# A graph layer on one core: from which chunk ScalarE and SyncE take over single gathers from GpSimd

## The chip, the cores and the metric

The kernel runs on one core of a Trainium2 chip. Its time is the device time of one launch in microseconds, as the median of the runs shown; before the change that is 15449.47 us (three runs, 15443.1 to 15450.64 us). The engines are named as the profile names them: PE (TensorE, matrix products), DVE (VectorE), ACT (ScalarE), POOL (GpSimd) and SP (SyncE, which only issues transfers here).

## The reference

A graph of 50,000 nodes with 160 features each and 1,650,000 edges, sorted by target. Each edge takes the row of its source node, multiplies it with four edge attributes and small weight matrices, and is summed into its target; then follow a residual, a ReLU and a layer norm.

```python
ss, vv = (s[src], v[src])                       # rows of the source nodes
out0 = C0 * (ss * e0 @ W1 + dot * INV3 @ W2)
out1 = C1 * (p3 + p4 + p5)                      # linear in the source row, too
m = jnp.concatenate([out0, out1.reshape(-1, 3 * MUL1)], axis=1)
m_agg = jax.ops.segment_sum(m, dst, num_segments=n)
...
return x + jax.nn.relu(h)                       # h: m_agg times Ws and Wv
x = _layernorm(x + _L0_gnn_ref(...), axis=-1)
```

Everything ahead of the ReLU is linear in the source rows, so the kernel first sums the rows times each of the four attributes (160 features times 4) and multiplies with one folded matrix per node afterwards.

## The kernel before

**Units, groups, pairs, chunks.** 128 edges are a unit, 6 units a group, 2 groups a pair (12 units), 10 pairs a chunk (120 units). There are 1044 pairs in 105 chunks, which the code numbers from 0, so the seventh chunk is chunk 6 and the third is chunk 2. Chunks 0 to 4 read their edges from the inputs; chunk 5 and later read them from a table `edges` in DRAM that the kernel writes itself, free of self loops.

**The way of a unit.** POOL gathers its 128 source rows with one indirect transfer (`gather`, line 459) into `xg`, a buffer of one pair, of which there are four (pool `rows`). So POOL can start pair p + 4 only when PE has done pair p. DVE builds the weighted one-hot matrices `ha` (`spread`, lines 474 and 477), PE multiplies (line 502), and DVE adds the result to the node sums (`turn_sums`, lines 518 and 527). When 128 nodes are complete, PE multiplies them with the folded matrix (line 822), DVE adds the residual rows `xt` and norms (lines 185 to 201), ACT takes a square root (line 195), SP loads `xt` ahead (line 765) and sends the result (line 920).

**Single rows.** Some units of a chunk are not gathered by POOL. A `Fetcher` of an engine fetches their 128 rows with 128 plain transfers of 640 bytes (line 376), whose addresses it loads into registers 32 at a time (line 372). `spots` holds the places in a chunk: units 38 and 98 for ACT, 104 for SP, before the change in chunks 2 to 103. DVE prepares the addresses (`list_rows`, lines 403 and 404). The rows of chunk s + 1 are handed out evenly (`deal`) over ten pairs from the fifth pair of chunk s on, so these transfers stand in the orders of ACT and SP between their other work. ACT writes into `xscalar`, SP into `xsync`.

**Packs.** The table `edges` is made in packs of 128 table rows, beside the main loop. SP reads a pack's edges (`read`, lines 596 to 600); ACT casts them to `prow` (`begin`, lines 604 to 606) and, three times, a third of the sources to `marks` (`count`, line 624); DVE marks and moves out self loops (lines 625 to 688); SP stores the table, in 16 rounds of 8 rows of 28,440 bytes (`edges<-prow`, each with 768 bytes `selves<-mine`; line 739, addresses loaded at line 722) and a short last round. There is one buffer `prow`: the cast that begins a pack waits until all stores of the pack before have landed. The first pack has to be stored before chunk 5 is loaded; later packs have some 1,400 us each.

**What sets the order.** On SP, PE, DVE and ACT the order of the code holds (`manual_schedule`), each engine waits in order, and work that belongs to a later pair is put in between the groups by `after_pair` and `work`; a pack's steps are spread evenly up to a due pair. Of eight semaphores, SP's other transfers each take the next one and wait until its last transfer has landed; single rows have their own semaphores and don't wait.

Of the kernel before, what the change touches and what calls it, by code (L numbers as in the profile page):

```python
# [39 lines left out]
F32 = mybir.dt.float32  # L40
I32 = mybir.dt.int32
# [3 lines left out]
ALU = mybir.AluOpType  # L45
AX = mybir.AxisListType
ET = mybir.EngineType
# [3 lines left out]
P = 128  # L51
MUL0, MUL1 = 64, 32
D = MUL0 + 3 * MUL1
# [10 lines left out]
W = 32  # L64
# [3 lines left out]
PG = 2  # L68
# [9 lines left out]
KM = WS - 1  # L78
REST = 15
LEAD = 3  # L80
BY_SCALAR, BY_SYNC = 2, 1
FBEGIN, FWAIT = 4, 4

def plan(n_nodes, n_edges):

    nblk = 125
    assert n_nodes % nblk == 0
    assert W == FB
    nb = n_nodes // nblk
    again = 9  # L90

    per_unit = P * n_nodes / n_edges
    group = max(g for g in range(1, 17)
                if g == 1 or (g + 0.2) * per_unit + 1 + 5 * math.sqrt(g * per_unit * per_unit / P) <= W)
    head = math.ceil(min(HEAD, n_edges / (group * P)) / SG) * SG
    eh = head * group * P
    row = group * P * 3 // 2 + math.floor(per_unit * group * 3 / 2 * (1 - n_nodes / n_edges))
    assert row * n_nodes / n_edges + 5 * math.sqrt(row * n_nodes / n_edges / 16) < KM

    far = math.ceil(6 * math.sqrt(n_edges) / 2 * n_nodes / n_edges) + 2  # L100
    rows = math.ceil((n_edges - eh) / row) + 2
    ngroups = math.ceil((n_edges - n_nodes + eh * n_nodes / n_edges + far) / (group * P))
    assert eh + (rows - 1) * row - n_nodes + eh * n_nodes / n_edges - far >= ngroups * group * P
    units = P * math.ceil(max(math.ceil(n_edges / P) + again - 1, math.ceil((eh + rows * row + 1) / P)) / P)
    return nblk, nb, again, group, units, ngroups, row, head, rows, far
# [3 lines left out]
def tile_gnn_resnorm(ctx: ExitStack, tc: tile.TileContext, x, src, dst, attr, W1, W2, W3, W4, W5, Ws, Wv, out, n_edges):  # L109
    nc = tc.nc  # L110
    N = x.shape[0]
    NBLK, NB, GA, G, NU, NG, L, NH, NR, FAR = plan(N, n_edges)
# [107 lines left out]
    NSC = math.ceil(NG / SG)  # L220
# [12 lines left out]
    with tc.tile_pool(name="once", bufs=1) as once, tc.tile_pool(name="raw", bufs=2) as rawp, \  # L233
# [8 lines left out]
        spotp, ownp, listp, heldp, scalarp, syncp = (  # L242
            later_pools.enter_context(tc.tile_pool(name=name, bufs=bufs))
            for name, bufs in (("spot", 3), ("own", 2), ("list", 2), ("held", 1),
                               ("scalar", BY_SCALAR + 1), ("sync", BY_SYNC + 1)))
        extremes = once.tile([P, 2, NSC], F32, name="extremes")
        count_ = once.tile([1, SG], F32, name="count")
        nc.gpsimd.iota(count_, pattern=[[1, SG]], base=0, channel_multiplier=0, allow_small_or_imprecise_dtypes=True)
# [8 lines left out]
        per = SG // PG  # L257
# [92 lines left out]

        class Fetcher:

            def __init__(self, engine, et, pool, n, place):
                self.engine, self.et, self.pool, self.n = engine, et, pool, n
                self.rows, self.turn, self.left, self.asked = deque(), 0, 0, []
                self.landed = [tc.alloc_semaphore(f"{pool.name}{i}") for i in range(4 * (n + 1))]
                self.spots = [math.ceil((FBEGIN + per * (i + 1) / n + FWAIT - per) * PG * G) + place for i in range(n)]
                assert all(0 <= at < per * PG * G for at in self.spots)

            def prepare(self, s, line, at, u):  # L360

# [19 lines left out]

                self.rows.extend(partial(one, q, e) for q in range(P // W) for e in range(W))

            def begin(self, wanted):
                assert len(self.rows) == wanted * self.n * P
                self.left = len(self.rows)

            def deal(self, gone):
                keep = math.floor(P * self.n * (1 - gone))
                while self.left > keep:  # L390
                    self.rows.popleft()()
                    self.left -= 1

        fetchers = [Fetcher(*f) for f in ((nc.scalar, ET.Activation, scalarp, BY_SCALAR, 2), (nc.sync, ET.SP, syncp, BY_SYNC, 8)) if f[3]]
        wanted = [(f, at) for f in fetchers for at in f.spots]
        assert len({at for _, at in wanted}) == len(wanted)

        def list_rows(s, u0, ef):

            line = listp.tile([P, len(wanted), W], I32, name="line")  # L400
            held = heldp.tile([P, len(wanted), W], F32, name="held")
            for i, (f, at) in enumerate(wanted):
                nc.vector.tensor_scalar(held[:, i], ef[:, 0, (u0 + at) % NK], 0.0, float(N - 1), op0=ALU.max, op1=ALU.min)
            nc.vector.tensor_scalar(line, held, float(4 * D), None, op0=ALU.mult)
            for i, (f, at) in enumerate(wanted):
                f.prepare(s, line[:, i], at, u0 + at)

# [436 lines left out]
        spots = once.tile([1, 2 * npacks * RP], I32, name="spots")  # L844
# [10 lines left out]
        counts = once.tile([P, 2, npacks], F32, name="counts")  # L855
# [9 lines left out]
        def after_pair(p, f, *args):  # L865
            later.setdefault(p, []).append((f, args))
# [96 lines left out]
        def reach(s):  # L963

            end = min(NG, (s + 1) * SG) * G * P
            if s * SG < NH:
                return 0
            if s + 1 < NSC:
                end = max(end, (s * SG * G + P) * P)
            if s * SG == NH:  # L970
                end = max(end, (s * SG + W) * G * P)
            return end - EH

        packs, due = [], []
        for i in range(npacks):

            first = next(s for s in range(NH // SG, NSC)
                         if reach(s) > row_start(i * RP)[0][0])
# [23 lines left out]
        for p, (s, g, ng) in enumerate(pairs):  # L1002
            if (p + LEAD) % per == 0 and (p + LEAD) // per + 1 < NSC or not p:
                ahead_ = (p + LEAD) // per + 1
                end = reach(ahead_)
                assert end <= 0 or rows_stored[0] == NR or end <= row_start(rows_stored[0])[0][0]
                raws[ahead_] = load(ahead_)
            if p % per == 0 and s + 1 < NSC:
                after_pair(p + 1, do_cast, s + 1)
                after_pair(p + 2, do_place, s + 1)  # L1010
                if s + 2 == NSC:
                    after_pair(p + 4, examine_all)
                    after_pair(p + 6, read_flags)
            rows = gather(s, placed[s], (g - s * SG) * G, ng * G)
            for j, ps in enumerate(group_sums(p, rows, has.pop(p))):
                if j == 1 and turning:
                    turn_sums(*turning)
                    turning = None
                if j == 3 and p + 1 < len(pairs):
                    s1, g1, ng1 = pairs[p + 1]  # L1020
                    has[p + 1] = spread(placed[s1], (g1 - s1 * SG) * G, ng1 * G)
                work(1.0)
                if p % per == FBEGIN and not j:
                    begun_at = p
                    for f in fetchers:
                        f.begin(0 < s < NSC - 2)
                for f in fetchers:
                    if f.left:
                        f.deal((p - begun_at + (j + 1) / (ng * G)) / per)
                if packs and p >= START:  # L1030
                    when = p + (j + 1) / (ng * G)
                    todo = math.ceil(len(packs[0]) * min(1, (when - began) / max(1, due[0] - began)))
                    for step in packs[0][done:todo]:
                        if step:
                            step()
                    done = max(done, todo)
                    if done == len(packs[0]):
                        packs.pop(0), due.pop(0)
                        done, began = 0, when
            turning = p, ps  # L1040
            if p == START - 2:
                with ExitStack() as behind, tc.tile_pool(name="begin", bufs=1) as beginp:
                    for i in first_ones:
                        behind.enter_context(tc.issue_after(i))
                    weights(beginp, psM)
            if p == START - 1:
                with ExitStack() as behind, tc.tile_pool(name="table", bufs=1) as tablep:
                    for i in first_ones:
                        behind.enter_context(tc.issue_after(i))
                    row_table(tablep)  # L1050
                nc.gpsimd.iota(place_, pattern=[[1, L]], base=1, channel_multiplier=0,
                               allow_small_or_imprecise_dtypes=True)
                packp = later_pools.enter_context(tc.tile_pool(name="pack", bufs=1))
            hand_over(p)
# [20 lines left out]
    with tc.tile_pool(name="up", bufs=1) as up, tc.tile_pool(name="us", bufs=2) as us, tc.For_i(0, once_more, 1):  # L1075
# [18 lines left out]
        for s in range(nseg):  # L1094
# [7 lines left out]
            for c in range(CB):  # L1102
# [3 lines left out]
                at = us.tile([PB, 2, SEG], F32, name="at")  # L1106
# [5 lines left out]
        f = up.tile([PB, CB], F32, name="f")  # L1112
# [12 lines left out]
    with tc.tile_pool(name="edges2", bufs=2) as ep, tc.tile_pool(name="ops2", bufs=2) as op, \  # L1125
            tc.tile_pool(name="node2", bufs=1) as np_, tc.tile_pool(name="psA2", bufs=2, space=PSUM) as psA, \
            tc.tile_pool(name="psF2", bufs=1, space=PSUM) as psF:
        with tc.For_i(0, blocks, 1) as b:
# [35 lines left out]
            for h in range(2):  # L1164
# [3 lines left out]
                at = np_.tile([D // 2, NK, NBLK], F32, name=f"ac{h}")  # L1168
# [3 lines left out]
            i = 0  # L1172
# [44 lines left out]
```

## Time and profile before

| | us |
|---|---|
| median of three runs | 15449.47 |
| the profiled execution's own time | 15440.23 |
| its span, first to last instruction | 15438.1 |
| POOL busy in 12,216 gathers (line 459) | 11581.5 |
| PE busy | 10171.0 |
| DVE busy | 7652.8 |
| ACT busy | 171.5 |

A busy time counts only work of an engine itself; issuing transfers, which is all that SP does and most of what ACT does, isn't counted (SPq and ACTq in the rows). A row of the timeline has start, length, engine, line, operation, out<-in and a count, and in brackets how long the engine sat idle before it and what ended that. The window rows give for each stretch the busy time of the engines with the number of instructions, the granted clock of PE, the share of the DMA engines and GB/s.

### The profile page before, as it was taken

The page shows a single profiled execution, that of the slowest core. Times are in us where ns is not written, and L with a number is a line of the kernel's source. Part 1 is how long each engine was busy: PE and PEld are TensorE (multiplying, and loading weights), DVE is VectorE, ACT ScalarE, POOL GpSimd, SP SyncE. Part 2 cuts the span into 40 slices and gives each one's busy share as a digit, 9 for nine tenths or more (in the row PEclk, how much of TensorE's full clock was granted, in tenths as well). Part 3 has the DMA queues.
Part 4 walks back from the last instruction along what each step waited for, and adds up shares of the span by engine and source line. Part 5 has one row for each costly group of instructions (what it writes and reads, how often), then busy time and mean ns, then how long its engine had stood idle before and what let it go on. Part 6 is the DMA issues. An engine that isn't in the chain of part 4 may idle for free.

```text
span 15438.1 us, 175175 instructions
## 1 busy us (share of the span) xinstructions
PE 10171.0 (66%) x28971; PEld 6746.8 (44%) x28972; DVE 7652.8 (50%) x12634; ACT 171.5 (1%) x273; POOL 11585.0 (75%) x12229
## 2 busy tenths in 40 slices
PE   3466666666666666666666666666666666666666
PEld 3344444444444444444444444444444444444444
DVE  8465355435635553563455355435634553554333
ACT  0000000000000000000000000000000000000000
POOL 7677777777777777777777777777777777777777
PEclk6655555555555555555555555555555555555555
DMA  3333333333333333333333333333333333333332
GB/s 83 87 85 93 93 81 83 98 86 85 91 93 83 84 95 89 84 84 97 85 85 91 91 82 85 96 89 83 83 100 86 82 87 93 81 86 85 85 82 75
DMA packets 909328, 1346.94 MB, mean 87 GB/s; under 512 B 292862, under 2 KB 683298, under 8 KB 905526
## 3 DMA queue, kind: packets, MB, share of 16 engines
q0 software_dynamic: 586368, 1001.52, 25.4%
q1 hardware_dynamic: 268330, 316.48, 6.6%
q10 hardware_dynamic: 53488, 17.70, 0.6%
q14 instruction: 911, 7.46, 0.2%
q8 instruction: 231, 3.78, 0.1%
HBM read 1263.28 MB, written 71.42 MB: 86 GB/s over the span
## 4 chain that ended last, share of the span: by engine, by line
POOL 51%; issue 21%; DMA 19%; PE 4%; DVE 1%; SPq 0%; POOLq 0%; DVEq 0%
POOL xg L459 51%; DMA xg<-in_x,si 18%; PE ps L502 3%; DMA selves<-mine 1%; PE phb L822 0%; DVE ha L477 0%; SPq L739 0%; DVE prow L688 0%; DVE ring L527 0%; SPq L376 0%; DMA xt<-in_x 0%; DVE sums L518 0%; DVE hot L474 0%; DVE ring L813 0%; DVE xr L809 0%
## 5 line engine op out<-in xcount | busy, mean ns | idle before, releaser
L459 POOL DMA_INDIRECT xg<-in_x,si x12216 | 11581.5, 948 | 3831.6 <-issue 3491.8
L502 PE MATMUL ps<-xg,ha 128*128 128x160 f32 x24432 | 9418.3, 500 | 5253.2 <-DMA xg<-in_x,si 4659.5
L502 PEld LDWEIGHTS ps<-xg,ha 128*128 128x128 f32 x24432 | 5765.7, 292 | 8675.4 <-DMA xg<-in_x,si 7382.9
L518 DVE STREAM_TRANSPOSE sums<-ps 128x320 f32<-128x320 f32 x1044 | 536.1, 513 | 6766.0 <-PE ps L502 6736.7
L477 DVE TENSOR_TENSOR ha<-hot,pk 128x1536 f32<-128x1536 f32 x1044 | 1830.4, 1753 | 35.8
L822 PE MATMUL phb<-BWk,ring 128*128 128x160 f32 (+1 forms) x3910 | 1250.3, 417 | 0.0
L822 PEld LDWEIGHTS phb<-BWk,ring 128*128 128x128 f32 (+1 forms) x3910 | 1020.3, 294 | 0.0
L527 DVE TENSOR_TENSOR ring<-ring,sums 128x160 f32 x2087 | 684.5, 328 | 338.0 <-issue 202.3
L474 DVE TENSOR_TENSOR hot<-bank,rel 128x384 f32<-128x384 f32 x1044 | 573.1, 549 | 69.9 <-DMA xt<-in_x 68.1
L688 DVE COPY_PREDICATED prow<-marks,prow 128x2370 f32<-128x2370 int32 (+5 forms) x198 | 548.6, 2770 | 1.1
L813 DVE STREAM_TRANSPOSE ring<-xr 128x1280 f32<-128x1280 f32 x188 | 468.7, 2493 | 6.5
L688 DVE COPY_PREDICATED pra<-marks,pra 128x1580 f32<-128x1580 int32 (+5 forms) x198 | 377.1, 1905 | 0.0
L809 DVE TENSOR_TENSOR xr<-xr,bank 128x1280 f32<-128x1280 f32 x188 | 278.9, 1483 | 6.6 <-DVE bank L808 0.2
L185 DVE SCALAR_TENSOR_TENSOR y<-phb,xt 128x320 f32<-128x320 f32 x196 | 95.5, 487 | 256.7 <-PE phb L822 256.0
L195 ACT ACTIVATE rstd<-mv,eps_t 128x2 f32<-128x2 f32 x196 | 58.0, 296 | 14013.9 <-DVE mv L190 13216.5
L524 DVE TENSOR_TENSOR ring<-ring 128x196 f32<-128x196 f32 (+20 forms) x485 | 149.3, 374 | 1.8
L502 PE MATMUL ps<-xscalar,ha 128*128 128x160 f32 x408 | 146.9, 462 | 0.0
L201 DVE TENSOR_SCALAR o<-y,mv,rstd 128x160 f32<-128x160 f32 x391 | 130.8, 376 | 7.5
L685 DVE COPY_PREDICATED_SCALAR hit<-marks,none 128x395 int32 (+5 forms) x198 | 129.8, 655 | 7.0
L772 DVE MEMSET ring<- 128x1280 f32 (+1 forms) x98 | 119.3, 1218 | 22.6 <-issue 22.6
L189 DVE BATCH_NORM_STATS2 st<-y 128x6 f32<-128x160 f32 x391 | 121.6, 311 | 6.7
L686 DVE COPY_PREDICATED hit<-marks,pri 128x395 int32<-128x395 int32 (+5 forms) x198 | 118.2, 597 | 6.8
(353 smaller groups left out, 2187.4 us busy)
## 6 DMA issues: line engine op xcount, KB each, us to landing
xscalar<-in_x ACTq DMA_DIRECT2D x26112, 0.6 KB
xsync<-in_x SPq DMA_DIRECT2D x13056, 0.6 KB
xg<-in_x,si POOLq DMA_INDIRECT x12216
xr<-in_x SPq DMA_DIRECT2D x187, 640.0 KB
r<-edges SPq DMA_DIRECT2D x100, 384.0 KB
edges<-prow SPq DMA_DIRECT2D x1330, 27.8 KB
xt<-in_x SPq DMA_DIRECT2D x195, 160.0 KB
out<-o SPq DMA_DIRECT2D x195, 160.0 KB
```

The costliest lines, as they stand in the source:

```text
L201: nc.vector.tensor_scalar(o[:n, i], y[:n, i], mv[:n, i, 0:1], rstd[:n, i:i + 1], op0=ALU.subtract, op1=ALU.mult)
L459: nc.gpsimd.indirect_dma_start(out=xg[:, j, :], out_offset=None, in_=x, in_offset=bass.IndirectOffsetOnAxis(ap=placed[0][:, u + j:u + j + ...
L474: idle[:] = [nc.vector.tensor_tensor(hot[:, :n], slotsP[:, 0:W].unsqueeze(1).to_broadcast([P, n, W]), rel[:, u:u + n].unsqueeze(2).to_broa ...
L477: nc.vector.tensor_tensor(ha[:, :n], hot[:, :n].unsqueeze(2).to_broadcast([P, n, NK, W]), pk[:, :, u:u + n].rearrange("p k u -> p u k").un ...
L502: mm = nc.tensor.matmul(ps[:, j // G, :], ha[:, j].rearrange("p k w -> p (k w)"), xr, start=j % G == 0, stop=j % G == G - 1)
L518: nc.vector.transpose(at[:, :ng], ps[:, :ng].rearrange("p g (b f) -> p g b f", f=FB))
L524: nc.vector.tensor_tensor(ring[k][:, b, :past], ring[k][:, b, :past], ring[k - 1][:, b, S:S + past], op=ALU.add)
L527: nc.vector.tensor_tensor(here, here, at[:, i], op=ALU.add)
L688: nc.vector.copy_predicated(what[:n, a:e], mi[:, r].unsqueeze(2).to_broadcast([n, e - a, what.shape[2]]), what[:n, a + d:e + d])
L809: nc.vector.tensor_tensor(xr[:, :nq], xr[:, :nq], sumP[:, :nq].unsqueeze(2).to_broadcast([P, nq, D]), op=ALU.mult)
L813: nc.vector.transpose(ring[k][:, :, c0:c0 + nq * W].rearrange("p b (w q) -> p q b w", q=nq), xr[:, :nq].rearrange("p q (b f) -> p q b f", ...
L822: wrote("misc", nc.tensor.matmul(ph[:nb], ring[k][:, i, c0:c0 + nb], BWk[:, i, :], start=i == 0, stop=i == ND - 1))
```

## The change

ACT's fetcher starts with chunk 6 and SP's with chunk 8, where both started with chunk 2. How many units a chunk has for each (two and one), their places, the buffers and the semaphores stay; the lists of addresses are made only for chunks that have any. Lines after 243 move by up to nine.

```diff
-BY_SCALAR, BY_SYNC = 2, 1
+BY_SCALAR, SCALAR_FIRST = (2,), 6
+BY_SYNC, SYNC_FIRST = (1,), 8
...
-            def __init__(self, engine, et, pool, n, place):
...
-                self.spots = [math.ceil((FBEGIN + per * (i + 1) / n + FWAIT - per) * PG * G) + place for i in range(n)]
...
+            def spots(self, s):
+                n = self.counts[s % len(self.counts)] if self.first <= s < NSC - 1 else 0
+                ats = [math.ceil((FBEGIN + per * (i + 1) / n + FWAIT - per) * PG * G) + self.place for i in range(n)]
+                assert all(0 <= at < per * PG * G for at in ats)
+                return ats
...
-            def begin(self, wanted):
-                assert len(self.rows) == wanted * self.n * P
-                self.left = len(self.rows)
+            def begin(self, s):
+                assert not self.left and len(self.rows) == len(self.spots(s + 1)) * P
+                self.all = self.left = len(self.rows)
...
-        wanted = [(f, at) for f in fetchers for at in f.spots]
+            wanted = [(f, at) for f in fetchers for at in f.spots(s)]
+            if not wanted:
+                return
```

In the built program POOL has 12,230 gathers instead of 12,216: eight of ACT's units (chunks 2 to 5) and six of SP's (chunks 2 to 7) are now gathered. ACT issues 25,088 single rows instead of 26,112, SP 12,288 instead of 13,056.

On ACT, between the cast of chunk 4's edges and the cast that begins the second pack (pack 1), this stood before (`rf` are the edges as floats, `line` the addresses of single rows):

```order
L306 CAST ff<-fi 128x1
L307 CAST rf<-r_3741 128x256
L376 DMA xscalar<-in_x 1x640 x19
L372 TENSOR_LOAD line
L376 DMA xscalar<-in_x 1x640 x32
L372 TENSOR_LOAD line
L376 DMA xscalar<-in_x 1x640 x32
L372 TENSOR_LOAD line
L376 DMA xscalar<-in_x 1x640 x18
L604 CAST prow<-pri 128x1185
```

and this now:

```order
L307 CAST ff<-fi 128x1
L308 CAST rf<-r_2120 128x256
L613 CAST prow<-pri 128x1185
L614 CAST prow<-pri 128x1186
L615 COPY prow<-pra 128x1185x4
L633 CAST marks<-pri 128x395
```

The 101 single rows and their address loads are gone from ACT here. On SP, from the last whole row of the first pack (pack 0) to its short last round, before (`spots` are the addresses of table rows):

```order
L739 DMA edges<-prow 1x28440
L739 DMA selves<-mine 1x768
L376 DMA xsync<-in_x 1x640 x2
L372 TENSOR_LOAD line
L376 DMA xsync<-in_x 1x640 x5
L722 TENSOR_LOAD spots
L739 DMA edges<-prow 1x1152
L739 DMA selves<-mine 1x384
```

and now:

```order
L748 DMA edges<-prow 1x28440
L748 DMA selves<-mine 1x768
L731 TENSOR_LOAD spots
L748 DMA edges<-prow 1x1152
L748 DMA selves<-mine 1x384
```

The five to seven single rows that stood between any two rounds of stores of this pack are gone, with the address loads at each 32nd of them. The order of everything else on SP and ACT is unchanged.

More of the change, by code (lines that the diff above doesn't have):

```diff
@@ L244, in tile_gnn_resnorm @@
             for name, bufs in (("spot", 3), ("own", 2), ("list", 2), ("held", 1),
-                               ("scalar", BY_SCALAR + 1), ("sync", BY_SYNC + 1)))
+                               ("scalar", max(BY_SCALAR) + 1), ("sync", max(BY_SYNC) + 1)))
         extremes = once.tile([P, 2, NSC], F32, name="extremes")
@@ L351, in tile_gnn_resnorm, with __init__ @@
         class Fetcher:
-            def __init__(self, engine, et, pool, n, place):
-                self.engine, self.et, self.pool, self.n = engine, et, pool, n
-                self.rows, self.turn, self.left, self.asked = deque(), 0, 0, []
-                self.landed = [tc.alloc_semaphore(f"{pool.name}{i}") for i in range(4 * (n + 1))]
-                self.spots = [math.ceil((FBEGIN + per * (i + 1) / n + FWAIT - per) * PG * G) + place for i in range(n)]
-                assert all(0 <= at < per * PG * G for at in self.spots)
+            def __init__(self, engine, et, pool, counts, first, place):
+                self.engine, self.et, self.pool, self.counts, self.first, self.place = engine, et, pool, counts, first, place
+                self.rows, self.turn, self.all, self.left, self.asked = deque(), 0, 0, 0, []
+                self.landed = [tc.alloc_semaphore(f"{pool.name}{i}") for i in range(4 * (max(counts) + 1))]
+            def spots(self, s):
[3 more added lines that the diff above has]
+                return ats
             def prepare(self, s, line, at, u):
@@ L382, in prepare @@
                 self.rows.extend(partial(one, q, e) for q in range(P // W) for e in range(W))
-            def begin(self, wanted):
-                assert len(self.rows) == wanted * self.n * P
-                self.left = len(self.rows)
+            def begin(self, s):
+                assert not self.left and len(self.rows) == len(self.spots(s + 1)) * P
+                self.all = self.left = len(self.rows)
             def deal(self, gone):
-                keep = math.floor(P * self.n * (1 - gone))
+                keep = math.floor(self.all * (1 - gone))
                 while self.left > keep:
@@ L392, in deal @@
                     self.left -= 1
-        fetchers = [Fetcher(*f) for f in ((nc.scalar, ET.Activation, scalarp, BY_SCALAR, 2), (nc.sync, ET.SP, syncp, BY_SYNC, 8)) if f[3]]
-        wanted = [(f, at) for f in fetchers for at in f.spots]
-        assert len({at for _, at in wanted}) == len(wanted)
+        MOST = max(BY_SCALAR) + max(BY_SYNC)
+        fetchers = [Fetcher(nc.scalar, ET.Activation, scalarp, BY_SCALAR, SCALAR_FIRST, 2),
+                    Fetcher(nc.sync, ET.SP, syncp, BY_SYNC, SYNC_FIRST, 8)]
         def list_rows(s, u0, ef):
-            line = listp.tile([P, len(wanted), W], I32, name="line")
-            held = heldp.tile([P, len(wanted), W], F32, name="held")
+            wanted = [(f, at) for f in fetchers for at in f.spots(s)]
+            assert len({at for _, at in wanted}) == len(wanted)
+            if not wanted:
+                return
+            line = listp.tile([P, MOST, W], I32, name="line")
+            held = heldp.tile([P, MOST, W], F32, name="held")
             for i, (f, at) in enumerate(wanted):
                 nc.vector.tensor_scalar(held[:, i], ef[:, 0, (u0 + at) % NK], 0.0, float(N - 1), op0=ALU.max, op1=ALU.min)
-            nc.vector.tensor_scalar(line, held, float(4 * D), None, op0=ALU.mult)
+            nc.vector.tensor_scalar(line[:, :len(wanted)], held[:, :len(wanted)], float(4 * D), None, op0=ALU.mult)
             for i, (f, at) in enumerate(wanted):
@@ L1025, in tile_gnn_resnorm @@
                     for f in fetchers:
-                        f.begin(0 < s < NSC - 2)
+                        f.begin(s)
                 for f in fetchers:
```

## The prediction

> **What bounds the kernel.** I read the page's groups first, then stretches of one chunk each, then the waits and rows in the one stretch that stands out. The page's row of the gathers:
>
> ```profile
> L459 POOL DMA_INDIRECT xg<-in_x,si x12216 | 11581.5, 948 | 3831.6 <-issue 3491.8
> ```
>
> Busy and idle time together are 15413.1 of a span of 15438.1 us: POOL does nothing but gather, 0.95 us each and about 0.30 us of "issue" behind it, from start to end. So the time is the number of gathers by their pace, plus what makes POOL wait. POOL's windows, one for each of chunks 2 to 6 by the first gather of each (117 gathers, 118 where the next chunk's first is touched):
>
> ```profile
> 312.80:462.20 149.40, 110.88 (x118) 0.67 0.32 97
> 462.20:611.20 149.00, 110.59 (x118) 0.56 0.31 85
> 611.20:810.20 199.00, 110.87 (x118) 0.66 0.28 73
> 810.20:956.70 146.50, 110.71 (x117) 0.58 0.33 84
> 956.70:1103.70 147.00, 110.88 (x117) 0.58 0.32 83
> ```
>
> The same busy time in each, but chunk 4 takes 199.00 us where the two undisturbed chunks take 146.75 on average (1.254 us a gather). POOL's rows there:
>
> ```profile
> 624.93 0.95 POOL L459 DMA_INDIRECT xg<-in_x,si  x1 [0.30 <-issue]
> 640.47 0.94 POOL L459 DMA_INDIRECT xg<-in_x,si  x1 [14.59 <-PE ps L502]
> ...
> 654.22 0.95 POOL L459 DMA_INDIRECT xg<-in_x,si  x1 [0.30 <-issue]
> 688.87 0.95 POOL L459 DMA_INDIRECT xg<-in_x,si  x1 [33.70 <-PE ps L502]
> ```
>
> Two waits for a free `xg`, that is for PE: 14.59 + 33.70 less two usual gaps of 0.30 = 47.7 us. PE waits for DVE, and DVE for these:
>
> ```profile
> 563.44 0.69 DVE L527 TENSOR_TENSOR ring<-ring,sums 128x160 f32 x2 [1.99 <-issue]
> 632.25 0.56 DVE L474 TENSOR_TENSOR hot<-bank,rel 128x384 f32<-128x384 f32 x1 [68.13 <-DMA xt<-in_x]
> ...
> 672.70 0.84 DVE L625 TENSOR_TENSOR hit<-marks,prow 128x395 f32<-128x395 f32 x1 [36.69 <-ACT marks L624]
> ```
>
> First for the residual rows `xt`, which SP issues late, then for ACT's first cast to `marks` of pack 1. Why ACT is late:
>
> ```profile
> 520.82 0.41 ACT L307 CAST rf<-r 128x256 f32<-128x256 int32 x1
> 520.90 45.62 ACTq L376 DMA_DIRECT2D xscalar<-in_x  x101
> 663.82 2.28 ACT L604 CAST prow<-pri 128x1185 f32<-128x1185 int32 x1 [142.59 <-DMA edges<-prow]
> ...
> 672.17 0.49 ACT L624 CAST marks<-pri 128x395 f32<-128x395 int32 x1
> ```
>
> The cast to `prow` waits for the last store of pack 0, and three casts later comes `marks`, 8.35 us behind. Both DVE waits thus end at SP, whose rows at these two points are:
>
> ```profile
> 627.90 0.42 SPq L765 DMA_DIRECT2D xt<-in_x  x1
> 628.42 2.44 SPq L376 DMA_DIRECT2D xsync<-in_x  x6
> ...
> 640.01 1.79 SPq L376 DMA_DIRECT2D xsync<-in_x  x5
> ...
> 651.71 4.84 SPq L376 DMA_DIRECT2D xsync<-in_x  x7
> ...
> 662.50 0.23 SPq L739 DMA_DIRECT2D edges<-prow  x1
> ```
>
> SP works through pack 0's 16 rounds of stores, with 5 to 7 single rows ahead of each, and is behind: this is the only place where POOL loses much.
>
> **The change part by part.** *More gathers.* 14 units return to POOL: 14 x 1.254 = +17.6 us, on the path that sets the end, with nothing to hide them.
>
> *Fewer single rows on SP.* What a row costs is shown where SP's stores wait for earlier ones:
>
> ```profile
> 421.76 0.23 SPq L739 DMA_DIRECT2D edges<-prow  x1
> ...
> 456.54 0.23 SPq L739 DMA_DIRECT2D edges<-prow  x1
> ...
> 461.90 2.22 SPq L376 DMA_DIRECT2D xsync<-in_x  x7
> ...
> 475.77 0.23 SPq L739 DMA_DIRECT2D edges<-prow  x1
> ...
> 480.12 0.23 SPq L739 DMA_DIRECT2D edges<-prow  x1
> ...
> 480.80 1.56 SPq L376 DMA_DIRECT2D xsync<-in_x  x5
> 483.78 0.29 SPq L739 DMA_DIRECT2D edges<-prow  x1
> ...
> 492.33 0.23 SPq L739 DMA_DIRECT2D edges<-prow  x1
> ```
>
> From 475.77 to 480.12 are three stores, each issued when one four places ahead has landed: 1.45 us a store. The eight stores from 475.77 to 492.33 take 16.56 us, where eight by 1.45 are 11.6: the five single rows between cost 5.0 us, far above the 1.56 us of their issue, since the queue serves them in between. The eight before, from 456.54, with seven rows, took 19.23 us: 7.6 for the rows. Later the rows are cheaper and SP's own issue sets the round:
>
> ```profile
> 606.81 0.28 SPq L739 DMA_DIRECT2D edges<-prow  x1
> ...
> 615.19 2.92 SPq L376 DMA_DIRECT2D xsync<-in_x  x7
> ...
> 619.50 0.29 SPq L739 DMA_DIRECT2D edges<-prow  x1
> ```
>
> 12.7 us a round, of it 2.9 for the rows; without them 9.8, which is 1.22 us a store. So a store costs between 1.22 and 1.45 us once the rows are gone; I take 1.40, near the upper end, since stores still queue behind each other. The first store has landed at 421.76 (the fifth is issued then); the extra gathers ahead of it (one unit of chunk 2) shift that by 1.3. Pack 0 then needs 127 x 1.40 = 178 us more, and what else SP moves in between, from these rows:
>
> ```profile
> 512.96 0.78 SPq L270 DMA_DIRECT2D r<-in_src  x1
> ...
> 519.46 1.52 SPq L376 DMA_DIRECT2D xsync<-in_x  x2
> 522.39 0.29 SPq L739 DMA_DIRECT2D edges<-prow  x1
> ```
>
> some 9 us for chunk 4's edges (522.39 - 512.96, nearly all kept), 2 to 3 for one `out` and one `xt` (my estimate), 2 for the short round. That is 421.8 + 1.3 + 178 + 9 + 2.5 + 2 = 614.6, so ACT's cast starts at about 615 instead of 663.82. By 1.22 and 1.45 a store it is 592 and 621.
>
> *Is that early enough?* The cast's start leads POOL's second restart by 688.87 - 663.82 = 25.05 us. Without its waits POOL would have been there at 688.87 - 47.7 = 641.2; six more gathers (three each in chunks 2 and 3) make it 648.7. The cast must start by 623.6: the forecast has 9 us to spare, the upper bound 2.8. The wait for `xt` ends sooner by the same token (14 rounds: about 590 and its landing), so the first wait, POOL's at 626, goes as well. All 47.7 us are won back. If the cover fails, each us past 623.6 is one us of POOL.
>
> *Small losses.* Chunks 2, 3 and 4 took 2.65, 2.25 and (without the 47.7) 4.55 us more than 146.75: together 9.5, POOL waiting for its own landings while the queues were full. With no single rows between 0 and 9.5 come back; the stores remain, so I take half, 4.7.
>
> *ACT.* Its 1,024 rows fewer shorten nothing by themselves: POOL doesn't wait for ACT elsewhere. This one goes, too:
>
> ```profile
> 698.98 0.49 ACT L624 CAST marks<-pri 128x395 f32<-128x395 int32 x1 [22.92 <-issue]
> ```
>
> 54 rows stood ahead of that cast; POOL didn't wait then, so it is worth nothing. DVE's shorter lists (four short instructions a chunk) lie beside POOL's gathers: nothing.
>
> *Sum.* Against the profiled execution's own 15440.2 us: 15440.2 + 17.6 - 47.7 - 4.7 = 15405.4. The median of the runs shown lies 9.2 us above that execution, so 15414.6, a change of -34.8 us or -0.23%.
>
> The page "DMA: Bandwidth & Descriptors" of the Trainium skill (section "Issuing engines are not separate DMA queues") says that transfers of all engines run on the same 16 DMA engines, and that issuing elsewhere saves only the sequencer's time, usually small beside the transfer. Read for this change: taking rows off SP frees only their issue time. The five rows that cost 5.0 us for 1.56 us of issue speak against that small price in the early rounds, the later rounds for it; it is the first rival below.
>
> **The rivals.** *Only SP's issue time is freed.* The chain of waits up to the `xt` landing passes through SP all along:
>
> ```profile
> by line: DMA selves<-mine 45.7%; SPq L739 14.8%; SPq L376 8.3%; DMA xt<-in_x 7.5%; issue 5.4%; SPq L722 4.3%; DMA out<-o 3.1%; DMA r<-in_attr 2.9%; SPq L372 2.6%; DMA edges<-prow 2.4%; SPq L270 1.5%; SPq L276 0.9%; SPq L600 0.3%; DVE hot L4
> ```
>
> This is from 404 to 632.3 us; single rows and their address loads have 8.3 + 2.6 = 10.9% of 228 = 24.9 us of it, and the three groups behind it 2.4 + 1.8 + 4.8 = 9.1. The cast then starts at 663.8 + 1.3 - 34 = 631, 7.5 us too late: 15422. For it: half of the rounds look like the later ones. Against: the 5.0 us of five rows.
>
> *Slower: the stores set SP's pace, not the rows.* If the stores fill the time that the rows leave (the "DMA selves<-mine" share of the chain, 45.7%, is stores waiting for stores), the cast stays at about 664. POOL's later need (6 x 1.254 = 7.5 us) shortens the wait to 40.2: 15449.5 + 17.6 - 7.5 = 15459.6, slower. This decides as soon as the cast starts after about 654 (623.6 and the 30.1 that 47.7 less 17.6 leave). Against it: 16.56 us with five rows, 19.23 with seven.
>
> The Trainium skill's "Perfetto Trace Analysis" (section "DMA Optimizations") advises to spread transfers over the engines that can issue them where descriptor generation binds, which POOL's rows look like. By that alone the change costs its 14 gathers, the side of this rival.
>
> *A new wait.* When ACT and SP start in chunks 5 and 7 their rows could delay casts or `xt` there. The old kernel had the same rows in these chunks and POOL lost nothing (146.50 and 147.00), so 15465 and more (all of the 17.6 with the old wait kept) needs two mishaps.
>
> **How the numbers follow.** Forecast, wait gone: 62%, 15408 to 15420 by the small losses and the run's own spread. Only issue time or part of it: 22%, 15420 to 15440. Stores set the pace: 11%. Anything else, new waits among it: 5%. A measurement tells 0.2%, 31 us, from no change, so faster needs 15418.6 or less: most of the first case and little of the second, 0.56; slower by that needs over 15480: 0.03; the rest 0.41. The range for 8 in 10 is 15402 to 15446; the forecast's own is 15408 to 15420.
>
> **What would show it.** In the changed profile: 12,230 gathers at 1.25 us; no POOL wait over 5 us in chunk 4 and a length of about 152 us for 120 gathers; the cast to `prow` starting near 615 with an idle time before it that is about 45 us shorter; rounds of stores of some 11.3 us. Wrong would be the price of a store if the cast starts after 624 with the rows gone, the price of a gather if chunks 2 to 5 take more than 1.26 us a gather without waits, and the whole reading if POOL still waits 30 us for PE there.

## The result and the profile after

The changed kernel takes 15406.19 us (median of nine runs, 15401.8 to 15414.09), the kernel before beside it 15443.1 us (nine runs, 15439.35 to 15450.64): a ratio of 0.9975 with a 95% interval of 0.9966 to 0.9984. That is 36.9 us less; 34.8 were forecast. The profiled execution took 15404.57 us with a span of 15402.8.

The page's row of the gathers, and POOL's windows for chunks 2 to 6 by the first gather of each (here 120 gathers are a chunk; the last row has 118), in the kernel after:

```profile
L468 POOL DMA_INDIRECT xg<-in_x,si x12230 | 11593.9, 948 | 3782.0 <-issue 3511.0
```

```profile
312.50:462.80 150.30, 113.47 (x120) 0.66 0.35 99
462.80:613.00 150.20, 113.64 (x120) 0.56 0.35 94
613.00:763.30 150.30, 113.74 (x120) 0.62 0.36 92
763.30:913.40 150.10, 113.57 (x120) 0.58 0.31 75
913.40:1061.40 148.00, 112.01 (x118) 0.56 0.33 81
```

Chunk 4, which took 199.00 us, is now as long as its neighbours, at 1.2525 us a gather. What POOL waited for in that stretch, by the table of waits (total, times, longest):

```profile
POOL xg L468 <- issue: 35.0, 115, 0.3
POOL xg L468 <- PE ps L511: 1.5, 5, 0.3
```

The waits of 14.59 and 33.70 us for PE are gone. Upstream, ACT's rows and SP's. First ACT:

```profile
597.73 2.28 ACT L613 CAST prow<-pri 128x1185 f32<-128x1185 int32 x1 [114.82 <-DMA edges<-prow]
```

The cast that begins pack 1 starts 66.1 us earlier than at 663.82, still as soon as the last store of pack 0 has landed. SP's timeline from the first store of pack 0, the first stores of five later rounds, and the request for `xt`:

```profile
406.03 0.31 SPq L748 DMA_DIRECT2D edges<-prow  x1
...
414.81 0.23 SPq L748 DMA_DIRECT2D edges<-prow  x1
416.85 0.23 SPq L748 DMA_DIRECT2D edges<-prow  x1
...
433.53 0.26 SPq L748 DMA_DIRECT2D edges<-prow  x1
...
443.76 0.26 SPq L748 DMA_DIRECT2D edges<-prow  x1
...
454.38 0.26 SPq L748 DMA_DIRECT2D edges<-prow  x1
...
537.09 0.26 SPq L748 DMA_DIRECT2D edges<-prow  x1
...
547.66 0.26 SPq L748 DMA_DIRECT2D edges<-prow  x1
...
568.06 0.42 SPq L774 DMA_DIRECT2D xt<-in_x  x1
```

A round of eight takes 547.66 - 537.09 = 10.57 us, 1.32 us a store, and the two early ones shown take 10.2 and 10.6 us. The residual rows `xt` are asked for at 568.06 instead of 627.90. DVE waits for both as before, and shorter:

```profile
572.53 0.56 DVE L483 TENSOR_TENSOR hot<-bank,rel 128x384 f32<-128x384 f32 x1 [10.78 <-DMA xt<-in_x]
...
606.60 0.85 DVE L634 TENSOR_TENSOR hit<-marks,prow 128x395 f32<-128x395 f32 x1 [30.31 <-ACT marks L633]
```

The second wait still lasts 30.31 us, but it now ends at 606.60, while POOL still has free buffers of `xg`: four pairs of lead, 48 gathers of 1.25 us. It costs nothing.

### The profile page after: what moved, and what is told of

Same layout as the page of the kernel before. It is cut to its first block, busy times and chain, and to the rows that moved or that the text cites. A ratio compares the mean times of both kernels' runs of the same rounds, so it can differ in the third digit from the quotient of the medians.

```text
span 15402.8 us, 171527 instructions
## 1 busy us (share of the span) xinstructions
PE 10200.3 (66%) x28971; PEld 6755.8 (44%) x28972; DVE 7650.5 (50%) x12616; ACT 171.3 (1%) x273; POOL 11597.4 (75%) x12243
## 4 chain that ended last, share of the span: by engine, by line
POOL 53%; issue 23%; DMA 19%; PE 5%; DVE 1%; POOLq 0%
POOL xg L468 53%; DMA xg<-in_x,si 19%; PE ps L511 4%; PE phb L831 0%; DVE ha L486 0%; DVE ring L822 0%; DVE ring L536 0%; DVE sums L527 0%; DVE xr L818 0%; DVE hot L483 0%; DVE prow L697 0%; DVE ring L781 0%; DVE pri L692 0%; DVE spots L590 0%; DVE marks L690 0%
## 5 line engine op out<-in xcount | busy, mean ns | idle before, releaser
L468 POOL DMA_INDIRECT xg<-in_x,si x12230 | 11593.9, 948 | 3782.0 <-issue 3511.0
L483 DVE TENSOR_TENSOR hot<-bank,rel 128x384 f32<-128x384 f32 x1044 | 573.4, 549 | 12.6 <-DMA xt<-in_x 10.8
```

Source lines behind the costliest of these rows:

```text
L468: nc.gpsimd.indirect_dma_start(out=xg[:, j, :], out_offset=None, in_=x, in_offset=bass.IndirectOffsetOnAxis(ap=placed[0][:, u + j:u + j + ...
L483: idle[:] = [nc.vector.tensor_tensor(hot[:, :n], slotsP[:, 0:W].unsqueeze(1).to_broadcast([P, n, W]), rel[:, u:u + n].unsqueeze(2).to_broa ...
```

## The experiments

Each kernel is an edit of the changed one and runs beside the kernel before on the same chip. They ran on four chips, whose times differ: on the chips of f1 to f5 and of h1 the kernel before takes 15457.49 and 15451.99 us, but on those of e1 to e4 and g1 to g3 21269.54 and 21178.94 us. Ratios are of runs on one chip, and durations inside chunks 2 to 4 are taken from the chips of some 15450 us. What the two others show is told last.

**One engine early.** The forecast put the whole delay of the stores on SP's single rows and held ACT's for harmless. So one engine alone starts with chunk 2 again. e1 and f1 are the same kernel on two chips, and so are e2 and f2.

```diff
-BY_SCALAR, SCALAR_FIRST = (2,), 6
+BY_SCALAR, SCALAR_FIRST = (2,), 2
```

for e1 and f1, and for e2 and f2

```diff
-BY_SYNC, SYNC_FIRST = (1,), 8
+BY_SYNC, SYNC_FIRST = (1,), 2
```

> The changed kernel with ScalarE's single rows back from chunk 2 on; SyncE's stay from chunk 8. 12,222 gathers, 8 fewer than the changed kernel, 10 us by 1.25 each. Theory 'SyncE's rows are what delays the first pack': its stores land 1.31 to 1.40 us apart, ACT's cast to prow starts at 600 to 622, POOL has no wait over 5 us in chunk 4, and the time is about 15396 us (before: 15443, the change: 15406). Rival 'single rows of either engine fill the transfer queues': a store costs 1.45 or more, the cast starts after 630 and POOL waits over 8 us there: 15405 us or more.

> The changed kernel with SyncE's single rows back from chunk 2 on; ScalarE's stay from chunk 6. 12,224 gathers. Theory 'SyncE's rows are what delays the first pack': the cast to prow starts at 640 to 660, POOL waits 15 to 40 us for PE in chunk 4, each us of the cast past about 621 being one of POOL; the time is 15413 to 15438 us. Rival 'ScalarE's rows are what matters': cast before 622, no wait, 15399 us.

> The kernel of e1 again (ScalarE's single rows from chunk 2, SyncE's from chunk 8), since that chip ran every kernel some 37% slower and the first pack's stores took 290 to 340 us with and without rows. On a chip where the kernel before takes about 15443 us: by 'SyncE's rows are what delays the first pack' a store costs 1.31 to 1.40 us, the cast to prow starts at 600 to 622, POOL has no wait over 5 us in chunk 4, 15396 us. By 'rows of either engine fill the queues' the cast starts after 630 and POOL waits over 8 us: 15405 us or more.

> The kernel of e2 again (SyncE's single rows from chunk 2, ScalarE's from chunk 6). On a chip where the kernel before takes about 15443 us: by 'SyncE's rows' the cast starts at 640 to 660, POOL waits 15 to 40 us for PE in chunk 4, one us for each us of the cast past about 621: 15413 to 15438 us. By 'ScalarE's rows' the cast starts before 622, no wait, 15399 us.

e1 took 21247.59 us (ratio 0.9988, 0.9968 to 1.0007), e2 21199.41 (0.9959, 0.9939 to 0.9979); on that chip the two don't tell the theories apart. f1 took 15426.39 us (0.998, 0.9971 to 0.999), f2 15434.0 (0.9985, 0.9975 to 0.9994). Both lie between the two kernels, and each has one POOL wait in chunk 4. ACT's and POOL's timelines of f1, with ACT alone early:

```profile
505.28 41.25 ACTq L381 DMA_DIRECT2D xscalar<-in_x  x101
628.83 2.28 ACT L613 CAST prow<-pri 128x1185 f32<-128x1185 int32 x1 [123.22 <-DMA edges<-prow]
```

```profile
652.79 0.94 POOL L468 DMA_INDIRECT xg<-in_x,si  x1 [13.10 <-PE ps L511]
```

And of f2, with SP alone early:

```profile
632.64 2.28 ACT L613 CAST prow<-pri 128x1185 f32<-128x1185 int32 x1 [135.84 <-DMA selves<-mine]
```

```profile
657.01 1.05 POOL L468 DMA_INDIRECT xg<-in_x,si  x1 [15.25 <-PE ps L511]
```

The cast stands at 663.8 with both engines' rows, 628.8 with ACT's alone, 632.6 with SP's alone and 597.7 with none. So taking SP's rows away is worth 35 us of it and taking ACT's away 31 more: each engine's rows hold up the stores, and neither half alone takes the whole wait away. ACT issues no store; its rows slow SP's. The first stores of six rounds in f1 show it:

```profile
437.67 0.26 SPq L748 DMA_DIRECT2D edges<-prow  x1
...
450.20 0.26 SPq L748 DMA_DIRECT2D edges<-prow  x1
...
462.47 0.26 SPq L748 DMA_DIRECT2D edges<-prow  x1
...
567.90 0.26 SPq L748 DMA_DIRECT2D edges<-prow  x1
...
578.51 0.26 SPq L748 DMA_DIRECT2D edges<-prow  x1
...
588.95 0.26 SPq L748 DMA_DIRECT2D edges<-prow  x1
```

While ACT issues rows (its 101 end at 546.5) a round takes 12.5 and 12.3 us with not one row on SP between the stores; once ACT sits in front of the waiting cast, 10.6 and 10.4. The two early rounds shown, the third and fourth of the pack, take 10.2 and 10.6 us in the changed kernel, so it is not their place in the pack that makes them long. The stores' packets of 28,440 bytes take 1.12 us in f1 while ACT issues and 1.06 us in the changed kernel; the rest of the delay lies between them, and by what path it comes is not shown. SP's rows cost mainly their issue. In f2 the rounds with rows look like this:

```profile
438.37 0.29 SPq L748 DMA_DIRECT2D edges<-prow  x1
...
447.07 2.73 SPq L381 DMA_DIRECT2D xsync<-in_x  x7
451.20 0.29 SPq L748 DMA_DIRECT2D edges<-prow  x1
```

12.8 us, of it 2.73 for the issue of seven rows; the remaining 10.1 is a round without rows. Over the whole of pack 0 the sixteen rounds take 184.2 us in the changed kernel and 214.6 in f2, 30.4 more, and the issue of the 96 rows among them takes 31.9. In sum SP's rows cost what their issue takes. Beside ACT's rows it is the same: the sixteen rounds take 215.3 us in f1 and 245.7 in the kernel before, 30.5 more.

Past about 617 us, each us of the cast is one us of POOL's wait: cast less wait is 663.82 - 47.7 = 616.1 before, 628.83 - 12.8 = 616.0 in f1, 632.64 - 14.95 = 617.7 in f2 (waits less the usual gap of 0.30).

**Both early, but out of chunks 3 and 4.** Only the lists of chunks 3 and 4 are emptied, whose rows are issued during pack 0's stores.

```diff
-                n = self.counts[s % len(self.counts)] if self.first <= s < NSC - 1 else 0
+                n = self.counts[s % len(self.counts)] if self.first <= s < NSC - 1 and s not in (3, 4) else 0
```

with both starts at 2 (e4 and f4, one kernel on two chips).

> Single rows of both engines from chunk 2 on as before the change, left out only in chunks 3 and 4, whose rows are handed out while the first pack is stored: 12,222 gathers. Theory: the cast starts at about 600 as in the changed kernel, no wait of POOL, and 8 gathers fewer than the changed kernel: 15396 us. Rival 'the rows of chunk 5, handed out from the middle of chunk 4 on, delay the second pack's casts': POOL waits there again, over 8 us, and the time is 15405 us or more.

> The kernel of e4 again (single rows of both from chunk 2, left out in chunks 3 and 4 only). On a chip where the kernel before takes about 15443 us: cast at about 600, no wait of POOL, 15396 us; by the rival (rows of chunk 5 delay the second pack's casts) POOL waits over 8 us there and the time is 15405 us or more.

f4 took 15413.83 us (0.9973, 0.9962 to 0.9984), 43.7 less than before with 12,222 gathers; e4 21223.62 (0.9976, 0.9956 to 0.9997). f4's cast starts at 597.73, as in the changed kernel, and POOL waits nowhere over 3 us, so the rival of chunk 5's rows did not come. POOL in the same three stretches as in the changed kernel (f4 gathers three units fewer in chunk 2, so these are not exactly its chunks):

```profile
312.50:462.80 150.30, 112.86 (x120) 0.67 0.36 99
462.80:613.00 150.20, 113.61 (x121) 0.55 0.35 94
613.00:763.30 150.30, 113.70 (x121) 0.61 0.37 87
```

The rows of two chunks cause the whole wait; the other four chunks from which the change takes rows have no part in it. f1 and f4 have equally many gathers and ran on one chip: 15426.39 - 15413.83 = 12.6 us, which is f1's wait of 12.8. Eight gathers fewer than the change should make 10 us, but the two kernels weren't run on one chip, and the intervals overlap.

**No single rows at all**, and ten chunks later.

```diff
-BY_SCALAR, SCALAR_FIRST = (2,), 6
-BY_SYNC, SYNC_FIRST = (1,), 8
+BY_SCALAR, SCALAR_FIRST = (2,), 200
+BY_SYNC, SYNC_FIRST = (1,), 200
```

in f5; in e3 the two starts are 16 and 18.

> No single rows at all: both starts lie behind the last chunk, POOL gathers all 12,522 units. On a chip where the kernel before takes about 15443 us: 292 more gathers than the changed kernel at 1.25 us are 365 us, 15771 us, by 'a gather costs its pace and nothing hides it'; by the rival 'single rows slow POOL's gathers by the queues they share' the gathers get faster than 1.25 us and it is under 15650 us. On a slow chip like the one before: if single rows are what is slow there, the time falls from 21270 to near 15771 us; if the whole chip is slow, it stays over 20000 us.

> The changed kernel with both starts ten chunks later (16 and 18): 12,260 gathers, 30 more than the changed kernel. Theory 'a gather on POOL costs its pace and nothing hides it': 30 x 1.25 = 37.6 us more than the changed kernel, 15444 us, and the cast and the waits of chunk 4 as in the changed kernel. Rival 'part of it lies under other waits of POOL': less than 25 us more, under 15431 us.

f5 took 15729.16 us (1.0177, 1.016 to 1.0193). The page's row of its gathers:

```profile
L468 POOL DMA_INDIRECT xg<-in_x,si x12522 | 11883.4, 949 | 3819.8 <-issue 3583.0
```

292 gathers more than in the change cost 15729.1 - 15404.57 = 324.5 us between the profiled executions, 1.11 us each and not 1.25. Most of the difference is in the waits: POOL's idle time beyond 0.31 us a gather adds up to 4.0 us in f5 and 53.5 in the changed kernel, scattered in pieces of at most 3 us. So a unit fetched as single rows spares POOL 1.25 us and costs it about 0.17 in waits; that leaves 1.08, near the 1.11 measured. e3 took 20842.49 us on its chip (0.9793, 0.9768 to 0.9817): faster, where slower was expected. That belongs to the other chips, below.

**The change on another chip, and more rows.** g1 is the changed kernel itself. g2 and h1 are f4 with two units for SP in every second chunk from chunk 8 on, g3 with two in every chunk.

```diff
-BY_SYNC, SYNC_FIRST = (1,), 2
+BY_SYNC, SYNC_FIRST = (1, 2), 2
...
-                n = self.counts[s % len(self.counts)] if self.first <= s < NSC - 1 and s not in (3, 4) else 0
+                n = self.counts[s % len(self.counts) if s >= 8 else 0] if self.first <= s < NSC - 1 and s not in (3, 4) else 0
```

g3 has `-1` in place of `s % len(self.counts)` there.

> The changed kernel itself, unaltered, beside the next two on the same chip. Where the kernel before takes about 15443 to 15457 us it is 0.25% faster, some 37 us; in its profile the cast to prow starts at 598 give or take 3 and POOL waits nowhere over 3 us.

> The kernel of e4 (no single rows in chunks 3 and 4 alone), and from chunk 8 on SyncE fetches two units in every odd chunk: 12,174 gathers, 56 fewer than the change. By 'a gather costs 1.25 us, and a unit of single rows 0.17 us in scattered waits of POOL' (the 50 us that the kernel without single rows has not, over 292 units): 56 x 1.08 = 60 us less than the changed kernel, 0.39%. Rival 'SyncE cannot keep up while a pack is stored' (an odd chunk's 256 rows take it about 100 of 147 us, stores and their addresses 6.5 us every 22): POOL waits over 10 us for PE in those stretches and the gain is under 30 us.

> As the one before, but two units for SyncE in every chunk from 8 on: 12,126 gathers, 104 fewer than the change; 112 us less than it by the same prices, 0.73%. Rival 'SyncE cannot keep up': 100 of 147 us for rows and 43 for stores leave nothing while a pack is stored; POOL waits in each of the ten stretches of stores and it is slower than the one before.

> The kernel of g2 again, since that job met the slow chip. Where the kernel before takes 15443 to 15457 us: 12,174 gathers, 42 fewer than before the change and no wait of 48 us in chunk 4; by 1.08 us a unit 42 x 1.08 + 48 = 93 us less than before, 0.60%. Rival 'SyncE cannot keep up while a pack is stored': POOL waits over 10 us for PE in those stretches (from 1400 us on), and it is less than 60 us faster than before.

Against 21178.94 us for the kernel before, g1 took 21096.01 (0.9954, 0.9937 to 0.997), g2 22085.63 (1.0427, 1.0402 to 1.0452) and g3 24728.12 (1.1678, 1.1652 to 1.1703). h1, the same kernel as g2 on a chip that takes 15451.99 us for the kernel before, took 15381.47 (15378.74 to 15395.9; ratio 0.9955, 0.9942 to 0.9969), 70.5 us less and not the 93 expected. The change took off 36.9 in its own comparison; the two intervals still touch, so that h1 beats it is likely and not shown. On the other chip the same code is slower than both. What it lost against the expectation is in POOL's waits, which are 93.1 us beyond the usual gap in place of 53.5. The longest stands behind one of DVE:

```profile
1871.61 0.94 POOL L468 DMA_INDIRECT xg<-in_x,si  x1 [11.17 <-PE ps L511]
```

```profile
1850.09 0.19 DVE L816 TENSOR_TENSOR sa<-sa,bank 128x32 f32<-128x32 f32 x1 [35.90 <-DMA sa<-selves]
```

Pack 1's last store is issued at 1814.88, so this is not a wait while a pack is stored, as the rival had it. DVE waits for `sa`, rows of the table of self loops, which SP asks for only at 1832.21 and 1836.39, behind 32 single rows among others; in f4, with one unit for SP, DVE waits 7.8 us there. SP does fall behind, but with its loads.

## Why the prediction was right, and where not

- **The sum.** Forecast for the profiled execution 15405.4 us, measured 15404.57. The large terms hold: 14 gathers at 1.25 us, and the 47.7 us of waits, all gone. The likeliest case was the one that came, and the range held it. The median of 15406.19 us lies 2 us below the forecast's own 15408 to 15420, as the kernel before, too, ran 6.4 us faster than the median that the forecast started from.
- **What bounds the kernel.** Right. POOL's count of gathers, its pace and its waits account for the span in every kernel on the two chips of 15450 us; the chain from the last store to the cast to DVE to PE to POOL is shown by three casts (before, f1, f2) that move the wait one for one.
- **"ACT: its 1,024 rows fewer shorten nothing by themselves".** Wrong, and the step that would have failed a smaller change: those issued during pack 0's stores are worth 31 us of the cast's start, about 0.1 us for each of some 300. Had they stayed, as in f1, the cast would have stood at 628.8, past the forecast's own threshold of 623.6. That all of the wait went is thus in part luck: the change happened to take ACT's rows away as well. The forecast looked for ACT's effect at ACT, where POOL indeed waits for nothing; it is in the stores of SP, 1.57 us each in f1's first rounds against 1.32 in undisturbed ones (12.53 / 8 and 10.57 / 8).
- **The price of a row on SP, 5.0 us for five.** Measured correctly in a trace in which both engines issue rows, and then given to SP alone. Over the whole pack the price is the issue time, 0.33 us a row in f2, which is the first rival's. The Trainium skill ("DMA: Bandwidth & Descriptors", "Issuing engines are not separate DMA queues") says that starting transfers on several engines at once saves only the time that the sequencer takes to start them; f2's 31.9 us of issue for 30.4 us of delay agree with the rival's reading of it. But the rival's result, 15422, assumed that ACT's rows do nothing, too. Had the change moved SP's rows alone, that is f1: 13 us of wait would have stayed. Why SP's rows cost 1.0 us each in the early rounds, beside ACT's, and less in the later ones is left open; the two delays of the cast simply add up (31.1 and 34.9 us of 66.1).
- **The price of a store.** 1.40 us was taken, 1.32 measured (bounds 1.22 to 1.45). With 127 stores that is 10 us, and the first store had landed sooner (fifth issued at 416.85, not 423.1), 6 us, since seven single rows ahead of the pack's first store are gone, which the forecast did not count (first store at 406.03, in f2 at 411.82): together the cast at 597.7 instead of 614.6, the lead 20 us and not 9. The upper bound rested on three stores, from 475.77 on, beside which ACT was still issuing (until 478.9).
- **The threshold.** 623.6 was forecast; f1 and f2 give 616 and 618, where the same working (1.254 us for each of their two and four more gathers in chunks 2 and 3) gives 618.6 and 621.1. The working counted the gathers that are added in chunks 2 and 3, and not the small losses that come back there: chunk 4 begins at 609.98 in f1 and at 612.05 in f2, where 611.18 before and the added gathers make 613.7 and 616.2. In the changed kernel it begins at 613.02, so the threshold there is about 618.
- **Small losses.** Half of 9.5 us was taken. Chunks 2 to 4 took 497.4 us by the quoted windows and take 450.8 now; these three chunks now have nine gathers more (120 for 117 in each), 11.3 us, so 46.6 + 11.3 - 47.7 = 10.2 us came back besides the waits: all of the 9.5. Later some 5 us are given back: by the start of chunk 8 POOL is 41.1 us ahead (1209.0 against 1250.1), at the end of the span 35.3, of which 1.9 are a longer tail after the last gather; the rest is within the spread of the runs. The two errors cancel in the sum; a part of its accuracy is luck.
- **The rival on the slower side,** stores that fill what the rows leave, needed a cast after 654; it came at 597.7. **A new wait** in chunks 5 to 7 didn't come: chunk 5 takes 150.10 us for 120 gathers.

## What to carry to other kernels

A price read from a trace holds for the traffic in it: before giving it to one queue, ask which other engines were issuing beside it, since small transfers of another engine can slow the large ones, too. Where two causes delay the same point, look for both before counting on the whole wait: here each half left 13 to 15 us of 48, and only two chunks' rows mattered. A unit taken off the bounding engine is worth its pace less what its transfers do to the rest, some 1.1 us of 1.25 here, and this can change sign from one chip to the next.

## What the runs showed of the hardware

On two of the experiments' four chips the kernel before takes about 37% longer, and what it waits for is another. The page's row of the gathers, and PE's timeline, from g1, the changed kernel:

```profile
L468 POOL DMA_INDIRECT xg<-in_x,si x12230 | 11584.2, 947 | 9467.2 <-PE ps L511 4603.8
```

```profile
908.76 0.42 PE L511 MATMUL ps<-xg,ha 128*128 128x160 f32 x1 [2.50 <-issue]
911.56 0.42 PE L831 MATMUL phb<-BWk,ring 128*128 128x160 f32 x1 [2.38 <-issue]
913.66 0.42 PE L831 MATMUL phb<-BWk,ring 128*128 128x160 f32 x1 [1.68 <-issue]
916.46 0.42 PE L511 MATMUL ps<-xg,ha 128*128 128x160 f32 x1 [2.38 <-issue]
```

A gather takes 0.95 us as on the other chips; what grew is POOL's idle time (9467.2 us against 3782.0), most of all its waiting for PE. In such stretches PE starts an instruction 2.80, 2.10 and 2.80 us after the last, multiples of 0.70 us, with "issue" ahead of each: the profile shows nothing that it waits for. The granted clock is no lower (0.620 against 0.578). ACT is slowed likewise; its single rows in g1, and in the changed kernel on the first chip:

```profile
1494.45 88.32 ACTq L381 DMA_DIRECT2D xscalar<-in_x  x128
1582.89 103.96 ACTq L381 DMA_DIRECT2D xscalar<-in_x  x128
```

```profile
972.70 49.52 ACTq L381 DMA_DIRECT2D xscalar<-in_x  x128
```

0.69 to 0.81 us a row instead of 0.39. An estimate from these rows: a chunk's 256 rows take ACT 177 to 208 us there, where a chunk of g1 has 21094 / 105 = 201. The longest row of ACT's waits, in g1 and then in the changed kernel on the first chip, fits that:

```profile
ACT rstd L196 <- issue: 17921.6, 171, 154.3
```

```profile
ACT rstd L196 <- DVE mv L191: 13455.5, 186, 94.7
```

In g1 ACT goes from one square root to the next issuing rows, with nothing else to wait for; on the first chip it has time to wait for DVE. ACT's issue, and with more rows SP's, would then be as much the bound as POOL, which fits that fewer single rows are faster there (e3) and more are much slower (g2, g3). That PE's own late starts are the bound is a rival that these runs do not separate; a kernel without any single rows wasn't run there. Why the engines issue so slowly on those chips is open: the packets of the instruction queue q14 take no longer (424 ns against 421 on average).
